# A fused attention and expert kernel: order of ACT's and DVE's work within the attention steps, Newton groups, and the work behind the steps

## The chip, the cores and the metric

The kernel runs on one core of one Trainium2 chip. The metric is the time of the kernel on the device in microseconds (us), taken as the median of several runs. Beside it there is one profiled execution, whose trace gives each instruction's engine, line, start and duration; times in such a trace count from the start of its span. The engines are named as the profile does: PE is TensorE, DVE is VectorE, ACT is ScalarE, POOL is GpSimd, SP issues most of the DMAs.

## What is computed

The input `x` is 16 blocks of 128 tokens with 512 features; `ctx` is 16 blocks of 128 context tokens with 128 features, which serve both as keys and values. There are 32 query heads and 8 key heads of 16 features each, so four query heads share a key head. Then comes a mixture of 32 experts, of which each token takes 8, and a shared expert. Cut to what matters, the reference is:

```python
q = layernorm(x)                                  # no scale, no bias, eps 1e-5
w = softmax(q_heads @ k_heads.T / sqrt(16))       # per block and head
x = x + w @ v_heads                               # keys and values are ctx
h = layernorm(x)
scores = sigmoid(h @ gate_weight.T)               # 32 experts in 8 groups
# the best 4 groups by their two best scores, then the best 8 experts of these,
# weights normalised to sum to 2.5
routed = sum over chosen e: weight_e * (silu(h @ w1_e.T) * (h @ w3_e.T)) @ w2_e.T
x = x + routed + (silu(h @ sw1.T) * (h @ sw3.T)) @ sw2.T
```

All inputs and the output are fp32.

## The kernel before

**Stages.** The attention (`attention_small`) takes the first part of the span; then the routing (`route` and `slot_tokens`) computes weights and token lists while PE does the shared expert; then the experts run one after the other on gathered tokens, and their outputs are added to the output in memory by indirect DMAs. The change touches the attention, the seam between it and the routing, and the two helpers for layer normalisation.

**Order.** The instructions of PE, DVE, ACT and POOL stand in each engine's queue in the order in which the program writes them (`tc.manual_schedule`, around L180). So the place of a call in the Python text is its place in the queue, and an instruction that waits holds up all that stands behind it on its engine. Semaphores between engines are put in by the framework from the tiles that instructions read and write. Two instructions of two engines that touch the same PSUM tile are put in order, also where both only read.

**The steps.** The loop goes over 32 steps n, one for each block b = n // 2 and each half i of its key heads. In step n, in this order:

- what is listed for the head of the step (`head[n]`): among it, at certain steps, the masked copies of keys on ACT (`keys`, L335), the normalised rows of a coming block on DVE (`rows_of`, L118), statistics for the layer norms on DVE (`layernorm_stats`, L91 and L92), Newton iterations for reciprocal square roots (`layernorm_rstd`), the rows for the gate (`gate_rows`, L118, on POOL or DVE, each followed by a DMA of 256 KB on SP's queue to `rows` in memory);
- `scores(n)`: PE multiplies queries and keys into two PSUM tiles `sc` (L442), ACT takes the exponentials to `p` (L452). The pool of `sc` has two buffers, both of which one step fills, so the scores of the next step wait for these exponentials;
- `values(n-1)`: PE multiplies the exponentials and values (L458) into `oT`, of which there is one buffer, and DVE copies it to `oTs` (L467);
- at some steps `gate_parts`: PE (L519) into the single buffer `lg`, ACT copies to `lgTs` (L528);
- `transposes(...)`: PE transposes up to two sets into one PSUM tile `x` of which there is one buffer (L415). The sets are the outputs of step n-2 (`added`), the queries of a coming block (`queries`, at even steps), or gate rows of a finished block (`turn_of`, from step 13 on). Then each set's follow-up is called in the order of the sets. For `added`, which comes first, it is a reciprocal (L476) and a product `at` (L478) on DVE and an addition to the block on POOL (L485); for the other two it is a copy by ACT, to `qT` (L433) or to `xnT` (L496);
- at some steps `gate_sums`: PE (L534) into `lg`, DVE copies to `logits` (L537);
- what is listed for the tail of the step.

At the heads of steps 8, 10, 12 and 14 stand squares of the context on ACT (L355) with a sum over them on DVE (L360); at 21 and 22 the longest key is found and compared with a bound.

**The seam.** After step 31 the last outputs are transposed, divided and added, the last blocks get statistics, Newton iterations, gate rows, transposes, gate parts and sums, in an order written out by hand (L640 to L671). `filler(n)` puts n matmuls of the shared expert (each a 512-column one, two instructions in the profile) between. Then `route` begins with ACT's sigmoid of `logits` (L1088) and 20 more such matmuls on PE, behind which PE counts the selected tokens (L1181).

Of the kernel before, what the change touches and what calls it, by code (L numbers as in the profile page):

```python
# [9 lines left out]
F32 = mybir.dt.float32  # L10
# [36 lines left out]
def tile_xattn_moe(  # L47
# [46 lines left out]
    def layernorm_rstd(first, n, eng=nc.vector):  # L94

        ve = xnp.tile([P, B], F32, tag="ve", name="ve")[:, 0:n]
# [3 lines left out]
            r, ve.bitcast(I32), -0.5, float(0x5F3759DF), ALU.mult, ALU.add  # L100
# [3 lines left out]
        for i in range(3):  # L104
            to = rstd[:, first : first + n] if i == 2 else r
            if eng is nc.vector:
                eng.scalar_tensor_tensor(h, r, -0.5, r, ALU.mult, ALU.mult)
                eng.tensor_tensor(h, h, ve, ALU.mult)
                eng.scalar_tensor_tensor(to, h, 1.5, r, ALU.add, ALU.mult)
            else:  # L110
                eng.tensor_tensor(h, r, r, ALU.mult)
                eng.tensor_tensor(h, h, ve, ALU.mult)
                eng.tensor_scalar(h, h, -0.5, 1.5, ALU.mult, ALU.add)
                eng.tensor_tensor(to, h, r, ALU.mult)
# [22 lines left out]
    FIRST = [*range(12), *range(15, 19)]  # L137
    SECOND = [*range(12, 15), *range(19, 2 * B)]
# [124 lines left out]
    def attention_small():  # L263


        with ExitStack() as ph:
# [86 lines left out]
            def key_lengths(k):  # L353
                sq = kpool.tile([P, 4 * KV, HD], F32, tag="sq", name="sq")
                nc.scalar.activation(  # L355
                    sq.rearrange("p k d -> p (k d)"),
                    cn[:, quarter[k], :].rearrange("p b e -> p (b e)"),
                    AF.Square,
                )
                nc.vector.tensor_reduce(kn[:, k, :], sq, AX.X, ALU.add)  # L360
# [41 lines left out]
            def transposes(*sets):  # L402


                x = ps_x.tile([P, 2, 2, 2, P], F32, tag="x", name="x")
# [18 lines left out]
                for s, (_, _, then) in enumerate(sets):  # L424
                    then(x[:, :, :, s])

            def queries(b):
# [3 lines left out]
                def then(x):  # L431
                    qTs[b] = ap2.tile([P, 2, 2, P], F32, tag="qT", name="qT")
                    nc.scalar.copy(qTs[b], x)  # L433
# [39 lines left out]
            def add(b, i, o):  # L473
# [11 lines left out]
                nc.gpsimd.tensor_tensor(part, part, at, ALU.add)  # L485

            def added(b, i):
# [3 lines left out]
                    lambda x: add(b, i, x.rearrange("p h r (g e) -> p (h r) g e", e=HP)),  # L491
                )

            def turn_of(b):
                def then(x):
                    nc.scalar.copy(  # L496
# [33 lines left out]
            def gate_sums(b):  # L530
                t = parts_of.pop(b)
                lg = ps_lg.tile([P, 2 * P], F32, tag="lg", name="lg2")[:, 0 : 2 * E]
                for i in range(2):
# [3 lines left out]
                nc.vector.tensor_copy(  # L537
                    logits[:, b : b + 2, :], lg.rearrange("p (b e) -> p b e", e=E)
                )
# [5 lines left out]
            head, tail = {}, {}  # L545

            def at_head(n, f, *a):
                head.setdefault(n, []).append((f, a))

            def at_tail(n, f, *a):  # L550
                tail.setdefault(n, []).append((f, a))


            for b in (2, 3):
                at_head(0, layernorm_stats, b, FIRST)
            at_tail(0, layernorm_rstd, 1, 3)
            at_tail(0, rows_of, 1)
            at_tail(1, rows_of, 2)
            for b, n in ((4, 1), (5, 1), (6, 2), (7, 2)):
                at_tail(n, layernorm_stats, b, FIRST)  # L560
            at_head(3, layernorm_rstd, 4, 4, nc.gpsimd)
            for b, n in zip(range(8, B), (5, 7, 8, 9, 11, 13, 14, 15)):
                at_head(n, layernorm_stats, b, FIRST)
            for b in range(3, B):
                at_head(2 * b - 3, rows_of, b)

            at_head(3, fixed_values, 1, nc.gpsimd)
            at_head(4, keys, 1, 0)
            at_head(5, keys, 1, 1)
            at_head(5, values_of, 1)  # L570
# [1091 lines left out]
```

## Time and profile before

| What | Value |
|---|---|
| median of 3 runs | 995.25 us (994.85 to 995.45) |
| the profiled execution's own time | 1000.62 us |
| its span | 998.8 us |
| mean granted PE clock | 0.991 of full speed |
| first scores (step 0) start | 10.49 us |
| scores of step 8, of step 31 start | 34.79 us, 111.21 us |
| sigmoid that begins the routing starts | 136.31 us |
| count of selected tokens starts on PE | 155.77 us |
| first expert's matmuls start | 234.04 us |

To read it: the span is the time between the profile's first and last instruction, and the execution's own time is a little longer. The profile's page first lists how busy each engine was, then the same in 40 slices of the span, here 25 us each, as tenths. Its chain of work follows the last instruction back to what released it, step by step. A line of the timeline is start, length, engine, line of the program, operation, the output and inputs by the program's names, and how many instructions were merged; the idle time ahead of it and what ended it stand in brackets. `PEld` is PE's loading of weights, which overlaps its matmuls. One matmul in fp32 appears as two instructions. A stretch of the windows view lists for each engine the busy time and the number of instructions, then the granted PE clock, the share of the DMA engines and GB/s.

### The profile page before, as it was taken

To read this page: it belongs to the slowest core of one execution; us is meant where nothing else is said; L and a number is where in the kernel's file an instruction comes from. 1 tells how busy PE (TensorE), PEld (TensorE's weight loads), DVE (VectorE), ACT (ScalarE), POOL (GpSimd) and SP (SyncE) were. 2 spreads that over 40 slices of the span, in tenths; PEclk is the share of its full clock that TensorE was granted. 3 is DMA by queue.
4 is the path that set the end of the run, shared out by engine and by line. 5 is a ranking of instruction groups with operands and counts; after the bars stand their busy time and mean duration, and the time that the engine had idled before them with its cause. 6 is when DMAs were issued, how large, how long until landed. Compare 5 with 4: busy or idle time off the path is not lost.

```text
span 998.8 us, 13920 instructions
## 1 busy us (share of the span) xinstructions
PE 972.1 (97%) x4965; PEld 550.6 (55%) x4965; DVE 286.9 (29%) x970; ACT 296.6 (30%) x466; POOL 488.4 (49%) x622
## 2 busy tenths in 40 slices
PE   8999899998999999999999999999999999999996
PEld 5334444545666556676666666667654444444453
DVE  6875668971211112121112111111111111211100
ACT  5777522421222212222222222222222222221221
POOL 3566432753445536444546454545464444455443
PEclk9999999999999999999999999999999999999998
DMA  9010104224767657667767676767675777666533
GB/s 310 19 46 36 61 22 179 65 89 145 171 133 170 139 132 186 144 150 182 160 149 164 152 160 156 163 166 180 133 171 151 154 169 185 144 160 164 120 66 45
DMA packets 59870, 137.16 MB, mean 137 GB/s; under 512 B 12168, under 2 KB 16392, under 8 KB 59792
## 3 DMA queue, kind: packets, MB, share of 16 engines
q0 software_dynamic: 32032, 69.25, 36.3%
q1 hardware_dynamic: 27680, 66.81, 19.7%
q8 instruction: 41, 0.67, 0.3%
q14 instruction: 37, 0.30, 0.1%
q10 hardware_dynamic: 80, 0.13, 0.0%
HBM read 96.71 MB, written 46.73 MB: 144 GB/s over the span
## 4 chain that ended last, share of the span: by engine, by line
PE 88%; issue 3%; POOL 2%; ACT 2%; DMA 1%; DVE 1%; another core or an unknown queue 1%; SPq 0%; POOLq 0%; ACTq 0%; DVEq 0%
PE gu L1474 44%; PE y L1528 22%; PE gu L244 6%; PE sc L442 4%; PE trx L1426 4%; PE oT L458 2%; POOL out_dram L1500 2%; PE y L1321 1%; PE x L415 1%; DMA out_dram<-yw,token 1%; ACT p L452 1%; PE tok L988 1%; DMA cn<-in_c_dram 1%; PE lgT L519 0%
## 5 line engine op out<-in xcount | busy, mean ns | idle before, releaser
L1474 PE MATMUL gu<-xnT,wup 128*128 128x256 f32 (+27 forms) x1664 | 492.1, 446 | 4.0 <-ACT xnT L1442 4.0
L1474 PEld LDWEIGHTS gu<-xnT,wup 128*128 128x128 f32 x1664 | 315.4, 191 | 197.1 <-issue 133.5
L1500 POOL DMA_INDIRECT out_dram<-yw,token x150 | 234.8, 1565 | 352.0 <-ACT yw L1537 245.4
L1528 PE MATMUL y<-wdn,sa 128*128 128x512 f32 (+2 forms) x672 | 263.3, 599 | 0.0
L1485 DVE TENSOR_TENSOR sa<-sl,gu 128x256 f32<-128x256 f32 (+27 forms) x104 | 52.2, 502 | 602.3 <-PE gu L1474 571.4
L1537 ACT ACTIVATE yw<-y,wt 128x512 f32<-128x512 f32 x138 | 94.8, 687 | 250.2 <-PE y L1528 201.5
L1402 POOL DMA_INDIRECT xg<-rows,token x138 | 142.3, 1031 | 47.8 <-issue 28.6
L1528 PEld LDWEIGHTS y<-wdn,sa 128*128 128x128 f32 (+2 forms) x672 | 98.0, 170 | 94.4 <-issue 85.0
L1483 ACT ACTIVATE sl<-gu 128x256 f32<-128x256 f32 (+27 forms) x104 | 46.7, 449 | 240.1 <-PE gu L1474 226.7
L1442 ACT COPY xnT<-trx 128x512 f32<-128x512 f32 x69 | 37.2, 589 | 99.4 <-PE trx L1426 84.8
L452 ACT ACTIVATE p<-sc 128x1024 f32<-128x1024 f32 x64 | 62.2, 1026 | 5.1 <-PE sc L442 4.9
L244 PE MATMUL gu<-xnT,sup 128*128 128x512 f32 x128 | 60.6, 613 | 0.7 <-ACT ssl L252 0.7
L982 POOL TENSOR_SCALAR hq<-slice_q,sq 128x138 f16<-128x138 f16 x32 | 35.2, 1114 | 34.6 <-DVE sq L1287 18.4
L442 PE MATMUL sc<-qT,kz 32*128 32x512 f32 x256 | 47.7, 640 | 4.1 <-ACT p L452 2.5
L1442 DVE COPY xnT<-trx 128x512 f32<-128x512 f32 x57 | 39.3, 689 | 31.7 <-PE y L1528 21.1
L1426 PEld LDWEIGHTS trx<-ident,xg 64*128 64x128 f32 x1104 | 37.2, 139 | 17.8 <-issue 17.5
L485 POOL TENSOR_TENSOR x<-x,at 128x256 f32<-128x256 f32 x32 | 23.3, 730 | 43.8 <-DVE at L478 43.7
L1426 PE MATMUL trx<-ident,xg 64*128 64x64 f32 x1104 | 42.1, 226 | 0.0
L244 PEld LDWEIGHTS gu<-xnT,sup 128*128 128x128 f32 x128 | 23.3, 194 | 24.5 <-issue 21.9
L458 PE MATMUL oT<-p,va 128*32 128x512 f32 x256 | 34.1, 605 | 0.0
L1457 DVE SCALAR_TENSOR_TENSOR own<-expert,owner,xg 128x32 f32<-128x32 f32 x138 | 31.4, 246 | 0.0
L1321 PE MATMUL y<-sdn,sa 128*128 128x512 f32 x64 | 29.3, 595 | 0.0
(186 smaller groups left out, 463.9 us busy)
## 6 DMA issues: line engine op xcount, KB each, us to landing
wup<-in_w_dram SPq DMA_DIRECT2D x64, 512.0 KB
wdn<-in_w_dram SPq DMA_DIRECT2D x32, 512.0 KB
rows<-xn SPq DMA_DIRECT2D x16, 256.0 KB
out_dram<-x SPq DMA_DIRECT2D x16, 256.0 KB
x<-in_x_dram SPq DMA_DIRECT2D x15, 256.0 KB
out_dram<-yw,token POOLq DMA_INDIRECT x150
xg<-rows,token POOLq DMA_INDIRECT x138
cTs<-in_cT_dram SPq DMA_DIRECT2D x4, 256.0 KB
```

The source lines that it names most:

```text
L244: nc.tensor.matmul(acc, lhsT=sup[:, w, d, ts(i, P)], rhs=xnT[k][:, d, :], start=(d == 0), stop=(d == ND - 1),)
L442: nc.tensor.matmul(scs[j // 2][:, j % 2], lhsT=kzs[b // 4 % 2][rows, b % 4, i, :], rhs=qT[rows], start=True, stop=True, tile_position=(j * ...
L452: nc.scalar.activation(p, sc, AF.Exp, scale=1.0 / HD**0.5)
L458: nc.tensor.matmul(oT[j * HP : (j + 1) * HP], lhsT=vas[b // 4 % 2][:, b % 4, 2 * j + i, :], rhs=ps.pop((b, i, j)), start=True, stop=True, ...
L1402: nc.gpsimd.indirect_dma_start(out=t, out_offset=None, in_=rows[:, :], in_offset=bass.IndirectOffsetOnAxis(ap=token[:, j : j + 1], axis=0) ...
L1426: nc.tensor.matmul(trs[s // 2][:, h, s % 2, d, :], lhsT=xg[j][rows_of_half, ts(d, P)], rhs=ident[rows_of_half, rows_of_half], start=True, ...
L1442: copy(xnT[n % NTB][:, :, col : col + P].rearrange("p d (h t) -> p h d t", h=2), tr)
L1474: nc.tensor.matmul(acc[:, 0:m], lhsT=wup[k % NW][:, w, d, ts(i, P)], rhs=xnT[n % NTB][:, d, 0:m], start=(d == 0), stop=(d == ND - 1),)
L1485: nc.vector.tensor_tensor(acts[n % NTB][:, i, 0:m], banks[2][:, 0:m], acc[:, 0:m], ALU.mult)
L1500: ins = nc.gpsimd.indirect_dma_start(out=flat, out_offset=bass.IndirectOffsetOnAxis(ap=token2[:, k - 1 : k] if a else token[0:b, j : j + 1 ...
L1528: nc.tensor.matmul(y[c0:c1, :], lhsT=acts[n % NTB][:, i, col : col + c1 - c0], rhs=wdn[pieces[n][0] % NW][:, i, :], start=(i == 0), stop=( ...
L1537: nc.scalar.activation(yws[j], y, AF.Copy, scale=wt[:, j : j + 1])
```

## The change

It has five parts.

1. In `transposes` the set of `added` comes last, so that ACT's copy of the other set is called first. Ahead of the last set's follow-up a new list, `between`, is run: what the new dictionary `middle` lists for the step. `rows_of` moves there from the heads (block b from the head of step 2b-3 to the middle of step 2b-4), the statistics of blocks 8 to 15 move there (odd steps 3 to 17), and the sums over squares too. In the last step the old order of sets is kept.
2. The copies of the first two blocks' queries go from ACT to DVE.
3. The squares go from steps 8 to 14 to steps 21 to 27; the longest key is found at 30 and compared at 31.
4. `layernorm_rstd` takes two iterations in place of three, with other constants, the second of higher order: on DVE 9 instructions in place of 11, on POOL 12 in place of 14. The groups are dealt out anew: on POOL four at steps 10, 16, 22 and 27 in place of five at 9, 15, 21, 27 and 31; that of step 31 goes to DVE.
5. The seam is written anew. The additions of the last four half blocks go from POOL to DVE, the gate rows of blocks 12 and 13 from DVE to POOL, the copies of the last logits from DVE to ACT, the transposes all go through `transposes` (two sets in a tile, some in a buffer of the `sc` pool), `gate_parts(8)` goes from step 31 behind it, and of the eight fillers two stand ahead of the last sums and six behind, where five and three stood.

```diff
@@ layernorm_rstd
+        c1, c2 = 0.703952253, 0.703952253 * 2.38924456
+        if eng is nc.vector:
+            z = xnp.tile([P, B], F32, tag="z", name="z")[:, 0:n]
+            eng.scalar_tensor_tensor(h, r, -c1, r, ALU.mult, ALU.mult)
+            eng.tensor_tensor(h, h, ve, ALU.mult)
+            eng.scalar_tensor_tensor(r, h, c2, r, ALU.add, ALU.mult)
+
+            eng.scalar_tensor_tensor(h, r, 0.375**0.5, r, ALU.mult, ALU.mult)
+            eng.tensor_tensor(z, h, ve, ALU.mult)
+            eng.scalar_tensor_tensor(h, z, -1.25 / 0.375**0.5, z, ALU.add, ALU.mult)
+            eng.scalar_tensor_tensor(to, h, 1.875, r, ALU.add, ALU.mult)
...
@@ transposes
-            def transposes(*sets):
+            def transposes(*sets, pool=ps_x, between=()):
...
                 for s, (_, _, then) in enumerate(sets):
+                    if s == len(sets) - 1:
+                        for f, a in between:
+                            f(*a)
                     then(x[:, :, :, s])
@@ queries
-                    nc.scalar.copy(qTs[b], x)
+                    (nc.scalar.copy if b > 1 else nc.vector.tensor_copy)(qTs[b], x)
@@ add
-                nc.gpsimd.tensor_tensor(part, part, at, ALU.add)
+                eng.tensor_tensor(part, part, at, ALU.add)
@@ what the steps hold
-            for b, n in zip(range(8, B), (5, 7, 8, 9, 11, 13, 14, 15)):
-                at_head(n, layernorm_stats, b, FIRST)
+            for b, n in zip(range(8, B), range(3, 18, 2)):
+                at(middle, n, layernorm_stats, b, FIRST)
             for b in range(3, B):
-                at_head(2 * b - 3, rows_of, b)
+                at(middle, 2 * b - 4, rows_of, b)
...
             for k in range(NTB):
-                at_head(8 + 2 * k, key_lengths, k)
-            at_head(21, longest)
-            at_tail(21, longest_turned)
-            at_tail(22, compare_lengths)
+                at(head, 21 + 2 * k, squares, k)
+                at(middle, 21 + 2 * k, key_lengths, k)
+            at(head, 30, longest)
+            at(tail, 30, longest_turned)
+            at(head, 31, compare_lengths)
...
-            for n, group in ((9, (8, 7)), (15, (15, 7)), (21, (22, 3)), (27, (25, 3)), (31, (28, 2))):
-                at_head(n, layernorm_rstd, *group, nc.gpsimd)
+            for n, group in ((10, (8, 7)), (16, (15, 6)), (22, (21, 4)), (27, (25, 3))):
+                at(head, n, layernorm_rstd, *group, nc.gpsimd)
+            at(head, 31, layernorm_rstd, 28, 2)
@@ the loop
                 sets = []
-                if n > 1:
-                    sets.append(added(*items[n - 2]))
                 if n % 2 == 0 and 0 < n // 2 < B - 1:
                     sets.append(queries(n // 2 + 1))
                 if n in turned:
                     sets.append(turn_of(turned[n]))
+                if n > 1:
+                    sets.append(added(*items[n - 2], nc.gpsimd if n < N - 1 else nc.vector))
+                if n == N - 1:
+                    sets.reverse()
+                between = middle.get(n, ())
                 if sets:
-                    transposes(*sets)
+                    transposes(*sets, between=between)
@@ the seam
+            for b in (12, 13):
+                gate_rows(b, nc.gpsimd)
+            gate_parts(8)
+            values(*items[N - 1])
+            layernorm_stats(14, SECOND)
+            transposes(added(*items[N - 2], nc.vector), turn_of(11), pool=ps_sc)
...
+            transposes(added(*items[N - 1], nc.vector))
+            layernorm_stats(15, SECOND)
+            layernorm_rstd(SECOND[14], 2)
+            nc.scalar.activation(table, table, AF.Sigmoid)
+            gate_sums(8, nc.scalar.copy)
+            transposes(turn_of(12), turn_of(13))
             gate_parts(10)
             filler(1)
-            gate_sums(10)
+            gate_sums(10, nc.scalar.copy)
...
             filler(1)
             gate_parts(12)
-            filler(2)
             gate_rows(15, nc.vector)
+            transposes(turn_of(15), pool=ps_sc)
             gate_rows(14, nc.vector)
+            transposes(turn_of(14, nc.vector.tensor_copy))
+            gate_sums(12, nc.scalar.copy)
...
             gate_parts(14)
-            gate_sums(14)
-            filler(3)
+            gate_sums(14, nc.scalar.copy)
+            filler(6)
```

## The prediction

> **What bounds the kernel now.** I read the page's engine shares first, then the chain of work that ended last, then the waits of the attention stage and its timeline. The page:
>
> ```profile
> PE 972.1 (97%) x4965; PEld 550.6 (55%) x4965; DVE 286.9 (29%) x970; ACT 296.6 (30%) x466; POOL 488.4 (49%) x622
> ...
> DVE  6875668971211112121112111111111111211100
> ACT  5777522421222212222222222222222222221221
> ```
>
> DVE and ACT are loaded only in the first five slices (125 us), which the change touches; there all engines pass work round within 3 us. TensorE's 97% is no measure of fullness: a matmul that waits in the array counts as busy. The timeline of the end of attention step 4, step 5, and the start of step 6 shows what happens (start, length, engine, line; in brackets idle time and what ended it):
>
> ```profile
> 25.13 0.41 PE L415 MATMUL x<-ident,xq 64*128 64x64 f32 x8
> ...
> 25.58 0.26 DVE L476 RECIPROCAL ri<-x 128x16 f32<-128x16 f32 x1
> ...
> 25.94 0.42 DVE L478 TENSOR_TENSOR at<-x,ri 128x256 f32<-128x256 f32 x1
> 26.46 0.59 ACT L433 COPY qT<-x 128x512 f32<-128x512 f32 x1 [1.28 <-DVE at L478]
> ...
> 26.94 0.72 ACT L335 ACTIVATE kz<-cTs,odd 128x512 f32<-128x512 f32 x1
> ...
> 27.56 1.93 ACT L452 ACTIVATE p<-sc 128x1024 f32<-128x1024 f32 x2
> ...
> 28.63 2.04 PE L442 MATMUL sc<-qT,kz 32*128 32x512 f32 x8 [0.63 <-ACT p L452]
> ```
>
> Step 4's transposes end at 25.54. ACT is free and its copy's data are there, but it waits for DVE's product `at` (end 26.36). The exponentials behind it start late, and the next scores wait for the PSUM that they release and run 2.04 us in place of 1.07. The waits from 8 to 112 us (total, times, longest) say that this is the rule:
>
> ```profile
> DVE oTs L467 <- PE oT L458: 23.2, 16, 3.5
> ACT qT L433 <- DVE at L478: 11.8, 12, 1.4
> ...
> ACT xnT L496 <- DVE at L478: 4.1, 7, 1.0
> ```
>
> Sixteen us of ACT are lost behind `at`; DVE has 23 us of slack in front of `oTs`. In the seam after the steps, the stretches of windows show TensorE's clock halved for 6 us, after TensorE was under half busy from 114.7 to 121:
>
> ```profile
> 114.70:121.00 6.30, 3.00 (x35) 1.73 (x33) 4.18 (x11) 1.36 (x3) 3.18 (x12) 1.00 0.20 73
> ...
> 122.00:125.00 3.00, 2.51 (x13) 1.37 (x14) 0.00 (x0) 1.34 (x3) 0.00 (x0) 0.50 0.02 5
> 125.00:128.00 3.00, 3.00 (x7) 1.58 (x7) 0.64 (x2) 1.55 (x3) 0.00 (x0) 0.50 0.00 0
> ```
>
> From 136.02 (routing) to 212 the chain is TensorE almost without a gap, so there time is TensorE's work.
>
> **What the skill says.** "PSUM — Partial Sum Buffer", Terms: two engines on the same bank and quadrant at once are an error, "reads against reads included". That is why a copy and a product of different halves of one tile are put in order; the trace agrees (copy 0.10 us after `at` ends, each time), so the change can only turn that order round. "TensorE: Matmul & The Clock Gate", HAM oscillation, asks for no idle gaps over about 3.4 us; here the clock fell with gaps of 1.5 us at most, so many short ones do it too. "GPSIMD Engine Reference", Engine selection, calls one-input work on GpSimd roughly line-rate; the trace does not agree: a normalisation is 2085 ns on POOL (x9), 549 to 671 ns on DVE.
>
> **The change, part by part.** *(1) The loop's floor.* From sc(4) at 22.00 to sc(31) at 111.21 are 27 steps in 89.2 us. Their TensorE work at the rate of unstretched rows: scores 1.07 and values 1.00 each (55.9); transposes 0.65 in 23 steps with two sets, 0.40 in 4 with one (16.6); four gate parts of 0.43, four sums of 0.56, one turn of 0.27 (4.2). Together 76.7: 12.5 us are stalls, and more than that cannot come out of these steps.
>
> *(2) Copy first.* It can start 0.07 after the transposes and takes 0.59; the first half of the next scores is ready 0.60 after them, so the exponentials follow at once. In exchange DVE's reciprocal now waits for the copy: `ri` and `at` end at 0.07+0.59+0.09+0.36+0.42 = 1.53 us after the transposes, before 0.82. Behind them on DVE stand the tail's statistics and the next `oTs`; TensorE waits for `at` with the next transposes, which come 2.07 us later. Slack 0.54, if ACT is free when the transposes end. The pieces put between (rows 0.46, statistics 0.82, a key sum 0.68) run in that wait on even steps. On odd steps without a copy they come ahead of `ri`: `at` ends 0.10+0.61 (`oTs`)+0.82+0.36+0.42 = 2.31 us after the transposes began, and the next begin 0.40+2.07 = 2.47 after: no stall, barely. DVE per pair of steps: 2x(0.61+0.36+0.34)+2x0.82+0.46 = 4.7 us; ACT: 4x0.975+0.6 = 4.5, with a second copy 5.1; TensorE 5.19, with two two-set steps 5.44.
>
> Walked pair by pair, with 0.4 for each kz (0.72 us of ACT at heads 4, 5, 9, 11, 17, 19; unchanged) and 5.9 where ACT's sum passes TensorE's (squares, 0.64 each, now at 21 to 27 in place of 8 to 14): steps 8-9 from 6.78 to 5.6, 10-11 from 6.77 to 5.6, 12-13 from 6.31 to 5.4, 14-15 from 7.24 to 5.4 (a square leaves), 16-17 from 6.66 to 6.4, 18-19 from 6.42 to 5.9, 20-21 from 7.99 to 6.4 (`longest`'s stalled turn leaves for 30), 24-25 from 6.79 to 6.4, 28-29 from 6.70 to 6.4, the others nothing. Sum 8.2.
>
> *(3) The start.* qT(0) and qT(1) go to DVE (priced as `oTs`, DVE's copy of 128x512 from PSUM, 0.69). sc(0) could start at 9.1, but the first exponential follows `va`'s copy (its keys' DMA, end 9.96): 1.7 earlier than 11.67. DVE pays 0.69 and saves two Newton operations at a pitch of 0.20; sc(2) comes at about 14.4 (16.39). Then DVE, with eight statistics to do, binds: I walk sc(8) to 32.4 (34.79). Gain 2.4. Bounds: 0 (DVE late) to 2.4. Steps together 10.6; I take 9.3, the rest for handoffs not walked.
>
> *(4) Newton.* POOL 14 to 12 operations at 0.28 (0.56 less, five groups to four, later heads); hidden by POOL's slack of two steps: each `at` waits only for the add two steps back. If that cover goes, 3.3 us of Newton hold up an add, and through it statistics. The group (28,2) leaves POOL (113.01 to 117.09) for DVE: 9x0.20 = 1.8.
>
> *(5) The seam.* From sc(31), t, to the sigmoid at 136.31 were 25.1 us. After: DVE does `at` to t+1.3, statistics of 13 to 2.1, the length check 0.4, Newton 1.8, rows 11 to 4.8, `oTs` to 5.4; values(31) behind that on TensorE to 6.4. The four late adds now run on DVE (0.42 each, `at`'s row of that size; at most the 0.69 of a 128x512 one) in place of POOL 0.73 and its handoff; the last ends at 10.1, statistics 15 at 10.9, Newton at 12.7, rows 15 and 14 at 13.8 (131.6, so t+20.4, before). Rows 12 and 13 go to POOL: 2x2.09, to t+8.5, each with its 256 KB write on SP's queue, order unchanged; behind them on POOL only memsets that wait anyway. ACT, with logits' copies added (0.25 each, between DVE's 0.22 for them and ACT's 0.38 for 256 columns), and the single `lg` buffer give: turn 15 and 14 to 15.9, sums 12 to 15.8, parts 14 to 16.7, sums 14 to 17.8, sigmoid 18.1. A halved clock took 3.3 us from TensorE before (6.6 at half rate, partly beside other waits); I add 1.1, a third, between none and all of it: 19.2, 5.9 us less. But fillers went from five ahead of the sigmoid to two, and six after it in place of three; from there TensorE binds (count started at 155.77, its selection ended at 155.50), so 3x0.87 = 2.6 us come back. Net 3.3; with the clock's bounds 1 to 4.5, and with a us of unwalked waits either way 0 to 5.5.
>
> *(6)* The rest shifts whole: weights, gathers and writes start from routing. Sum 9.3+3.3 = 12.6 us. On the profiled execution's own 1000.62 (span 998.8) that is 988.0; the runs' median is 0.5% less, which changes 12.6 by 0.1. Forecast 995.25-12.6 = 982.7.
>
> **Rivals.** *Half the loop:* the late release of x and DVE's odd steps take TensorE's place as the stall; for it speaks the slack of 0.54 and the near 2.3 against 2.47, against it DVE's 23 us of slack. Loop 4.5 in place of 9.3: 987.5. *Better seam:* TensorE's gaps end sooner, the clock stays up: 1.1 of my allowance, and 2.5 of short waits: 979. *Slower:* ACT runs behind by d when the transposes end, so copy, sums and release of x all slip; TensorE then stalls d-0.54 in each of about 25 two-set steps. It ends slower than before from d = 1.14 us on (0.6x25 = 15, over the 12.6 by 2), a little over one exponential; at d = 1.3 it costs 19: 982.7+19 = 1001.7. ACT's 5.9 against 5.44 in steps 18 to 27 speaks for it, but that backlog is half a us. *No change:* the 13 us gather wait from 219.73 absorbs the gain, if its end is set by DMA and not by the token list: 995. Its transfers start from routing, which speaks against.
>
> **Numbers.** Forecast 0.55, half the loop 0.25, better seam 0.10, slower 0.06, no change 0.04. Faster by over 0.2% (2 us, about what a measurement can tell here) 0.90, same 0.04, slower 0.06. The range reaches from the better seam with the loop's undiscounted 10.6 (977.8, set to 977) to half the loop with the start's 2.4 gone too (989.9): 990.
>
> **What would show it.** The wait of ACT's copies for `at` gone, `ri` waiting for ACT in its place; sc(8) near 32.4, sc(31) near 102, the sigmoid near 121; scores of 1.07 and few of 2.04. Wrong would be: transposes that wait for `at` by over 0.3 us a step, a seam as long as 25 us, or a later gather wait grown by what was won.

## The result and the profile after

The changed kernel takes 985.95 us (median of 4 runs, 985.39 to 987.26), the kernel before on the same chip 995.35 (994.85 to 996.01): a ratio of 0.9907 with a 95% interval of 0.989 to 0.9924, so 9.4 us faster where 12.6 were forecast. The profiled execution took 987.26 us, its span 985.4. The page of the changed kernel, the lines that answer to those of before:

```profile
PE 966.0 (98%) x4985; PEld 548.8 (56%) x4985; DVE 288.7 (29%) x972; ACT 296.7 (30%) x468; POOL 486.6 (49%) x597
...
DVE  7877778961121111111112111111121111111100
ACT  5788513412222222222222222222221222222221
```

Almost nothing was removed: DVE and ACT have as many busy microseconds as before, only closer together in the first five slices. Where the time went is read from landmarks of the traces:

| | before | after | gain | forecast |
|---|---|---|---|---|
| scores of step 8 start | 34.79 | 32.79 | 2.00 | 2.4 |
| from there to the scores of step 31 | 76.42 | 71.17 | 5.25 | 8.2 |
| from there to the sigmoid | 25.10 | 20.86 | 4.24 | 5.9 |
| from there to the count on PE | 19.46 | 22.05 | -2.59 | -2.6 |
| count | 155.77 | 146.87 | 8.90 | |

(The forecast took 9.3 for the first two lines together.) The profiled execution gained another 4.5 us behind the count. That does not belong to the change: from the count to the end of the execution the 14 traces of this study take either 840.3 to 840.5 us or 844.8 to 846.1, and which it is does not go with the edits. In the nine long ones, that of before among them, ACT's first copy for the experts starts 2.9 us after the transposes that it reads instead of at once, TensorE then waits 4.0 to 4.3 us in place of 1.17, and behind this wait its granted clock is at half for 3.4 or 6.8 us. All eight traces taken on two of the chips are long and all four taken on two others short, and the kernel before itself takes 1001.13 and 1000.80 us on the former, 995.68 and 995.79 on the latter; what holds up that copy is open. The medians' 9.4 agree with the 8.9 at the count.

The stretch at steps 4 to 6 that the prediction showed, in the timeline of the changed kernel:

```profile
23.74 0.44 PE L434 MATMUL x<-ident,oTs 64*128 64x64 f32 x8
...
24.22 0.59 ACT L455 COPY qT<-x 128x512 f32<-128x512 f32 x1 [0.26 <-PE x L434]
...
24.70 0.73 ACT L349 ACTIVATE kz<-cTs,odd 128x512 f32<-128x512 f32 x1
...
25.34 1.94 ACT L474 ACTIVATE p<-sc 128x1024 f32<-128x1024 f32 x2
...
25.88 0.24 DVE L498 RECIPROCAL ri<-x 128x16 f32<-128x16 f32 x1
26.15 0.42 DVE L500 TENSOR_TENSOR at<-x,ri 128x256 f32<-128x256 f32 x1
...
26.72 0.46 PE L434 MATMUL x<-ident,oTs 64*128 64x64 f32 x8 [0.48 <-DVE at L500]
...
27.11 1.35 PE L464 MATMUL sc<-qT,kz 32*128 32x512 f32 x8
```

The transposes end at 24.18 and ACT's copy starts 0.04 us later (before: 0.92 after their end, held by `at`). The masked keys and the exponentials follow without a gap, and the scores of the next step come 3.00 us after those of this one, where 3.16 passed before. `at` now ends 2.4 us after the transposes, and the next ones wait 0.48 us for it; in all steps that wait comes twice, 0.7 us together. The waits from 8 to 104 us (total, times, longest) say the same for all steps:

```profile
ACT p L474 <- PE sc L464: 14.7, 22, 1.8
...
PEld sc L464 <- ACT p L474: 4.5, 12, 0.8
...
DVE ri L498 <- ACT qT L455: 3.4, 7, 1.0
...
DVE ri L498 <- ACT xnT L518: 1.0, 3, 0.5
...
PE x L434 <- DVE at L500: 0.7, 2, 0.5
```

ACT's 16 us of waiting for `at` are gone, and DVE waits 4.4 us for ACT in exchange, as forecast. The 16 us did not become 16 us of time: ACT's first line, its wait for scores, grew from 4.9 us to 14.7. What took the place of the old wait is seen in one plain pair of steps:

```profile
88.59 1.14 PE L464 MATMUL sc<-qT,kz 32*128 32x512 f32 x8
...
89.83 1.94 ACT L474 ACTIVATE p<-sc 128x1024 f32<-128x1024 f32 x2 [0.92 <-PE sc L464]
...
91.30 1.65 PE L464 MATMUL sc<-qT,kz 32*128 32x512 f32 x8
...
91.82 0.30 PEld L464 LDWEIGHTS sc<-qT,kz 32*128 32x128 f32 x4 [0.22 <-ACT p L474]
```

The exponentials begin 1.24 us after the scores' start, 0.10 after their end: both halves of the scores come ready together. So the second exponential ends at 91.77, 3.18 after the scores began, and the second half of the next scores, which needs its PSUM, loads at 91.82. TensorE was there at 91.30. The scores last 1.65 in place of 1.07 to 1.14, once in each pair. ACT waits for TensorE, then TensorE for ACT, and neither is full.

In the seam TensorE's clock falls as before, only elsewhere (windows; the column ahead of the last two is the granted clock):

```profile
106.00:109.00 3.00, 1.61 (x28) 0.73 (x24) 2.65 (x15) 1.14 (x2) 0.75 (x2) 1.00 0.00 0
109.00:112.00 3.00, 2.43 (x18) 0.80 (x20) 1.88 (x5) 0.86 (x2) 3.00 (x2) 0.55 0.36 135
...
115.00:118.00 3.00, 2.62 (x26) 1.21 (x27) 2.58 (x13) 2.29 (x6) 0.00 (x0) 0.69 0.02 5
```

The clocks shown are means over the windows. Narrower ones give 0.50 from 109.4 to 112.7 us and again from 116.2 to 119.5, and 1.00 between and beside them; before it is 0.50 from 121.3 to 128.0. So the clock is at half for 6.8 us in both kernels, in two pieces or in one.

### The profile page after: what moved, and what is told of

Same layout as the page of the kernel before. It is cut to its first block, busy times and chain, and to the rows that moved or that the text cites. A ratio compares the mean times of both kernels' runs of the same rounds, so it can differ in the third digit from the quotient of the medians.

```text
span 985.4 us, 13941 instructions
## 1 busy us (share of the span) xinstructions
PE 966.0 (98%) x4985; PEld 548.8 (56%) x4985; DVE 288.7 (29%) x972; ACT 296.7 (30%) x468; POOL 486.6 (49%) x597
## 4 chain that ended last, share of the span: by engine, by line
PE 86%; issue 5%; POOL 3%; DMA 2%; DVE 2%; ACT 1%; POOLq 0%; ACTq 0%; DVEq 0%
PE gu L1492 42%; PE y L1546 21%; PE gu L258 6%; PE trx L1444 4%; PE sc L464 4%; PE oT L480 3%; POOL out_dram L1518 3%; PE y L1339 2%; DMA out_dram<-yw,token 2%; PE x L434 2%; PE warm L329 1%; PE tok L1006 1%; PE lg L556 0%; PE lgT L541 0%; DVE st L91 0%
## 5 line engine op out<-in xcount | busy, mean ns | idle before, releaser
L464 PE MATMUL sc<-qT,kz 32*128 32x512 f32 x256 | 43.9, 640 | 0.2 <-ACT p L474 0.2
L507 POOL TENSOR_TENSOR x<-x,at 128x256 f32<-128x256 f32 x29 | 21.3, 740 | 38.6 <-DVE at L500 36.4
```

The costliest lines, as they stand in the source:

```text
L464: nc.tensor.matmul(scs[j // 2][:, j % 2], lhsT=kzs[b // 4 % 2][rows, b % 4, i, :], rhs=qT[rows], start=True, stop=True, tile_position=(j * ...
```

## The experiments

**First group: which part makes the gain.** The theory was that the order of the sets makes the loop's 5.25 us.

*Order alone.* The kernel before, with:

```diff
                 sets = []
-                if n > 1:
-                    sets.append(added(*items[n - 2]))
...
                     sets.append(turn_of(turned[n]))
+                if n > 1:
+                    sets.append(added(*items[n - 2]))
+                if n == N - 1:
+                    sets.reverse()
```

> The kernel before, with one edit: within a step ACT's copy set is dealt ahead of DVE's sums set (except in the last step). My theory: the order alone gives the loop's gain, steps 8 to 31 get shorter by 5 us (measured 5.25 with the whole change), so the time falls from 995.4 to about 990 (988.5 to 991.5), and ACT's wait for the product at (11.8 and 4.1 us) is gone. Rival: the rows and statistics that the change puts between, and the squares and the length search that it moves to the end, do it; then the order alone gives under 1.5 us (994 to 996), because on DVE the rows and statistics now stand ahead of the late product and hold TensorE's transposes.

*Order undone.* The changed kernel, with:

```diff
-                if n == N - 1:
-                    sets.reverse()
+                if n > 1:
+                    sets = sets[-1:] + sets[:-1]
```

> The changed kernel with DVE's sums set dealt first again in every step, all else as changed. My theory (the order makes the loop's gain): 5 to 7 us come back, 991 to 993, and ACT waits for the product at again by over 8 us between 8 and 104 us. Rival (the moved squares, rows and statistics make it): at most 1.5 us come back, 986 to 987.5.

*First copies alone.* The kernel before, with:

```diff
-                    nc.scalar.copy(qTs[b], x)
+                    (nc.scalar.copy if b > 1 else nc.vector.tensor_copy)(qTs[b], x)
```

> The kernel before with the first two query copies on DVE in place of ACT, nothing else. My theory of the start: the first exponential no longer stands behind two copies of 0.6 us, and sc(8) comes up to 2 us earlier, which stays to the end: about 993.4. Rival: DVE, which has eight statistics to do there, pays 0.69 us for each copy and binds, so that sc(8) comes at the old time or later: 995 to 996; the start's gain in the changed kernel then comes from the other moves (statistics later, shorter Newton groups).

*Seam alone.* The changed kernel with order, first copies and the steps' lists as before:

```diff
-            for b, n in zip(range(8, B), range(3, 18, 2)):
-                at(middle, n, layernorm_stats, b, FIRST)
+            for b, n in zip(range(8, B), (5, 7, 8, 9, 11, 13, 14, 15)):
+                at(head, n, layernorm_stats, b, FIRST)
...
-                at(middle, 2 * b - 4, rows_of, b)
+                at(head, 2 * b - 3, rows_of, b)
...
-                at(head, 21 + 2 * k, squares, k)
-                at(middle, 21 + 2 * k, key_lengths, k)
-            at(head, 30, longest)
-            at(tail, 30, longest_turned)
-            at(head, 31, compare_lengths)
+                at(head, 8 + 2 * k, squares, k)
+                at(head, 8 + 2 * k, key_lengths, k)
+            at(head, 21, longest)
+            at(tail, 21, longest_turned)
+            at(tail, 22, compare_lengths)
```

> The changed kernel with the attention steps as before: sums first, rows, statistics, squares and length search at their old steps, first copies on ACT; what stays of the change is the work behind the last step and the shorter Newton groups. My theory: the seam is worth its 4.2 us less the 2.6 us of fillers behind the sigmoid, so 995.4-1.6 = 993.8 (992.5 to 994.5). Rival: the seam's gain exists only because the steps before it leave DVE less behind; then sc(31) to the sigmoid stays near 25 us and, with 2.6 us of fillers added, the time is 995.4 to 998.

**Second group: what the order needs beside it, and the seam.** *Between undone*: the changed kernel with the first three removed and the first three added lines of the last diff (statistics and rows at their old heads), nothing else.

> The changed kernel with DVE's statistics of the next query blocks and its query rows put back to the heads of their old steps; copies first, squares and length search late, seam as changed. My new theory, after the order alone gained only 0.8 us: the order pays only if these pieces stand behind it; at a step's head they stand ahead of the product that now comes late, and one of them waits for x (at step 7 of the order-alone run the next scores came 2.9 us late). Then the start loses 2 to 3 us again and steps 8 to 31 about 1: 3 to 4 us over the changed kernel, 0.994 of the time before. Rival: the moved squares and length search are the second half of the gain, and the place of rows and statistics costs at most 1 us: 0.991 to 0.992.

*Squares back*: the changed kernel with the rest of that diff, squares and length search at their old steps.

> The changed kernel with the squares, their sums and the length search at their old steps (8 to 14, 21, 22); rows and statistics between, as changed. My theory: in the order-alone run steps 20 to 23 took 15.1 us against 12.6 in the changed kernel, because the search's turn on TensorE waits for DVE behind the late product; so 2 to 2.5 us of the gain come from moving it, less 0.4 that DVE saves behind the last step: 0.9925 of the time before. Rival: with the rows and statistics out of the way the search costs nothing at step 21, and ACT's squares lie as well at 8 to 14: 0.9905, as the changed kernel.

*Fill gaps*: the changed kernel with fillers moved (and the transposes of step 30 given a PSUM buffer ahead of them, so that the order of buffers fits):

```diff
             gate_parts(8)
+            x30 = ps_sc.tile([P, 2, 2, 2, P], F32, tag="sc", name="x")
...
+            filler(2)
             values(*items[N - 1])
             layernorm_stats(14, SECOND)
-            transposes(added(*items[N - 2], nc.vector), turn_of(11), pool=ps_sc)
+            transposes(added(*items[N - 2], nc.vector), turn_of(11), x=x30)
...
             gate_sums(8, nc.scalar.copy)
+            filler(1)
             transposes(turn_of(12), turn_of(13))
...
-            filler(6)
+            filler(3)
```

> The changed kernel with three of the six expert pieces that stand behind the sigmoid put into TensorE's idle stretches of the seam: two ahead of the last values (1.96 us idle there), one ahead of the turns of 12 and 13 (1.35 us idle). My theory: TensorE's work from the sigmoid on sets the end, so 3 x 0.87 = 2.6 us leave it, and the busy array keeps its clock, which gives the last values (1.93 us at the lowered clock, 1.06 in the run with the old steps) and the pieces their full rate: 2.6 to 4 us, 0.9865 to 0.988 of the time before. Rival: the pieces hold up the last values or the turns by their own length on TensorE's queue, and the chain through DVE and ACT to the sigmoid slips by it: 0 to 1 us gain, 0.990 to 0.991.

*Three Newton iterations*: the changed kernel with the old iterations and their constant (`for i in range(3)` with factors -0.5 and 1.5), its groups dealt as changed.

> The changed kernel with the three old Newton iterations in place of the two new ones, so two more small operations per group on DVE and POOL, their dealing as changed. My theory: POOL's are hidden by two steps of slack, and DVE's two groups stand at the start and twice in the seam on the path (0.20 us an operation): 0.4 to 1.2 us over the changed kernel, 0.991 to 0.992 of the time before. Rival: POOL's late rstd holds up the query rows, which now come one step earlier, and the loop loses more than 2 us: above 0.993.

**Third group: what bounds a plain pair.** *A piece ahead* and *a piece between*: in `scores` of the changed kernel, in blocks 4 to 14, with `j == 0` and `j == 1` in turn:

```diff
+                    if 4 <= b < 15 and j == 0:
+                        nc.scalar.copy(table, table)
                     nc.scalar.activation(p, sc, AF.Exp, scale=1.0 / HD**0.5)
```

> The changed kernel with one small ACT copy (0.2 us, a 128x1 table onto itself) ahead of the two exponentials of every step from 8 to 29. My theory of why a plain pair of steps takes 5.92 us and not TensorE's 5.44: the two halves of the scores come ready together, 1.23 us after they start, and the second half of the next scores waits for the second exponential; this is a chain from TensorE to ACT and back, in which ACT waits for the scores (14.7 us in all). A piece ahead of the exponentials falls into that wait: steps 8 to 31 stay within 0.3 us of the changed kernel's 71.2. Rival: ACT's throughput is the bound there, and each of the 22 pieces costs its 0.2 us: 74 to 75.6.

> The same small ACT copy between the two exponentials of every step from 8 to 29. The chain theory: it makes the second exponential 0.2 us later, and with it the second half of the next scores, in each pair that this chain bounds: 0.2 us in each of 6 to 11 pairs, so 72.4 to 73.5 us for steps 8 to 31. Throughput theory: the same as with the piece ahead, 74 to 75.6. If neither, and TensorE alone sets the pace: 71.2 in both.

*Turns between*: the changed kernel, with `scores` calling a function after its second matmul:

```diff
                 for j in range(NJ):
+                    if j == NJ // 2:
+                        between()
...
+            late = range(6, N - 2)
...
+                if n - 1 in late:
+                    scores(*items[n], lambda: turns(n - 1))
+                    rest_of(n - 1)
```

where `turns` holds the sets and the transposes of a step, and `rest_of` what stands behind them.

> The changed kernel with TensorE's transposes of the step before issued between the two halves of the scores of steps 7 to 30, Newton groups and rows on POOL a step later. Chain theory: the transposes fill TensorE's wait for the second exponential, the first exponential finds its half ready sooner, and a plain pair goes from 5.92 toward 5.44: up to 5 us off steps 8 to 31 (66 to 68 us). Rival: the four matmuls of the scores run side by side on four strips of rows; issued as two halves they no longer do, each half takes about the 0.7 us that a half took alone in the order-alone run, and a step gets longer by 0.3 to 1 us: 78 to 95.

**Last: a further version.** *Fill more*: the kernel with the gaps filled, and:

```diff
-                nc.vector.tensor_copy(
+                (nc.scalar.copy if (b, i) in items[-2:] else nc.vector.tensor_copy)(
                     t.rearrange("p g (h s) -> p h g s", h=2),
...
-            filler(1)
+            filler(2)
             transposes(turn_of(12), turn_of(13))
...
             gate_parts(14)
+            filler(1)
             gate_sums(14, nc.scalar.copy)
-            filler(3)
+            filler(1)
```

> The kernel with three pieces in the seam's gaps, and three things more: a second piece ahead of the turns of 12 and 13 (0.53 us idle there), one between the parts and the sums of 14 (0.54 us idle), so that one piece stays behind in place of three, and the copies oTs of the last two steps on ACT, which waits 3.0 us there, in place of DVE, which is busy for 2.5 to 2.8 of every 3 us. My theory: from the last scores to the count TensorE's work is all there is, less its idle time, about 2.0 us of which is left; the two pieces take 1.1 of it and the earlier chain through DVE some of the rest: 1 to 2 us, 0.9842 to 0.9852 of the time before, count at 139.5 to 140.5 us. Rival: each piece delays the chain by what it does not hide and ACT's copies push the copies xnT: 0.986 to 0.988, count at 141.5 or later.

**What they gave.** Times are ratios to the kernel before on the same chip, with their 95% intervals (0.001 is 1 us); the other columns are landmarks of the traces in us.

| run | ratio | sc(8) | sc(8) to sc(31) | to sigmoid | to count |
|---|---|---|---|---|---|
| before | 1 | 34.79 | 76.42 | 25.10 | 19.46 |
| after | 0.9907 (0.989, 0.9924) | 32.79 | 71.17 | 20.86 | 22.05 |
| order alone | 0.9992 (0.9983, 1.0001) | 36.26 | 74.62 | 25.71 | 19.46 |
| order undone | 0.998 (0.9969, 0.9991) | 33.59 | 77.86 | 19.17 | 22.05 |
| first copies alone | 0.9986 (0.9976, 0.9995) | 33.63 | 76.71 | 25.50 | 19.45 |
| seam alone | 0.995 (0.9934, 0.9966) | 34.31 | 76.39 | 19.16 | 22.05 |
| between undone | 0.9909 (0.9894, 0.9925) | 33.40 | 71.54 | 19.94 | 22.05 |
| squares back | 0.9915 (0.9899, 0.9931) | 32.72 | 74.18 | 22.27 | 22.04 |
| fill gaps | 0.9862 (0.9841, 0.9883) | 32.54 | 71.18 | 18.27 | 19.48 |
| three Newton | 0.9913 (0.9897, 0.9929) | 32.93 | 71.18 | 20.08 | 22.04 |
| a piece ahead | 0.9911 (0.9891, 0.9932) | 32.02 | 71.28 | 19.49 | 22.05 |
| a piece between | 0.991 (0.9893, 0.9926) | 32.06 | 71.75 | 20.99 | 22.05 |
| turns between | 1.0113 (1.0096, 1.013) | 32.65 | 90.40 | 20.36 | 22.05 |
| fill more | 0.9859 (0.984, 0.9878) | 32.13 | 71.18 | 18.18 | 19.56 |

The first column of landmarks moves with the start of the first step (8.80 to 9.56 us in the runs with the first copies on DVE). The second repeats to 0.03 us where nothing in these steps differs, but for the first copies alone, where it is 0.3 longer than before.

**The order needs company.** The expectation for the order alone fell: 0.8 us and not 5, as the rival beside it had it. Undone in the changed kernel it costs 7.3 us by the ratios (0.998 less 0.9907, some 2 either way) and 5.8 at the count, where 5 to 7 were expected, and ACT's copies `qT` wait 16.0 us for `at` again. Both are true, since the order alone opens two stalls that the rest of the change removes. The first is at step 7 of the order-alone run (timeline):

```profile
27.24 1.74 PE L442 MATMUL sc<-qT,kz 32*128 32x512 f32 x8
...
27.84 0.69 DVE L91 BATCH_NORM_STATS2 st<-x 128x6 f32<-128x512 f32 x1 [1.70 <-POOL x L485]
...
28.67 0.66 DVE L91 BATCH_NORM_STATS2 st<-x 128x6 f32<-128x512 f32 x1
...
29.46 0.51 DVE L118 TENSOR_SCALAR xq<-x,mv,rstd 128x512 f32<-128x512 f32 x1
29.89 0.68 DVE L467 COPY oTs<-oT 128x512 f32<-128x512 f32 x1
...
30.63 0.16 PEld L458 LDWEIGHTS oT<-p,va 128*32 128x32 f32 x8 [2.48 <-DVE oTs L467]
30.63 1.28 PE L458 MATMUL oT<-p,va 128*32 128x512 f32 x8 [1.65 <-DVE oTs L467]
...
32.89 2.04 PE L442 MATMUL sc<-qT,kz 32*128 32x512 f32 x8
```

Two statistics and a row stand ahead of `oTs` on DVE, and the first of them waits 1.70 us for POOL's addition. So the copy comes no sooner than before (29.89 against 29.83), though the scores come 1.39 us sooner; the values of the step wait for that copy, TensorE idles 1.65 us, and then its clock is at half (0.50 in a window from 31.4 to 34.7). 5.65 us pass from one step's scores to the next. With between undone the same pieces stand there, TensorE idles 1.14 us, the clock stays at 1.00, and it is 4.53. The other is at step 21, in the run with the squares and the search put back (timeline):

```profile
77.69 0.27 PE L387 MATMUL kT<-ident,km 128*1 128x128 f32 x1 [1.24 <-DVE logits L559]
...
79.40 1.94 PE L480 MATMUL oT<-p,va 128*32 128x512 f32 x8
```

The search's turn shares the single `lg` buffer with the sums, whose copy stands on DVE behind the product `at`, now late. TensorE idles 1.24 us there (0.41 in the kernel before, where `at` came early), and then its clock is lowered: the granted clock is 1.00 until 78.4 us, 0.50 from 78.6 to 81.8 and 1.00 again from 82.0, and values that take 1.06 us take 1.94. Steps 8 to 31 lose 3.0 us by it, 2.55 of them in steps 20 to 23. In the traces the moved squares and search are thus the second half of the loop's gain, as the rival in the second group had it; the place of statistics and rows is worth 0.4 us in steps 8 to 31 and 0.7 at the start (sc(8) less sc(0) 23.89 in place of 23.23). I had expected 3 to 4 from that, which the measured 0.9909 excludes. And the moves need the order: with the sums first they make steps 8 to 31 slower than before (77.86 against 76.42). By the traces, then, in steps 8 to 31 the order is worth 1.8 us in the kernel before and 6.7 in the changed one; all that the change moves beside it costs 1.4 under the old order and brings 3.5 under the new (74.62 less 71.17). But the trace with the squares back is of the slowest of its eight runs: 997.33 us at a mean clock of 0.987, where the median is 992.6 and five of the others had 0.992 or 0.993. By the ratios the search's place is 0.8 us with an interval of some 2 either way, so how much of the 3.0 us the other runs lost is open.

**The start.** The first copies alone give 1.4 us (0.5 to 2.4), of which the traces show 0.7 to 1.2 at sc(8), by which run of the old start it is set against (34.31 or 34.79). The steps 0 to 8 themselves stay as long (24.31 against 24.30): what the edit brings is an earlier first step (sc(0) at 9.32; 10.01 to 10.49 in the three runs with ACT's copies). The other us comes with the order: 24.29 from sc(0) to sc(8) without it, 23.23 with it. It needs the shorter Newton iterations too: with three it is 23.76, since DVE's row at step 5 then waits 1.16 us for POOL's group in place of 0.63, and the step takes 3.53 us in place of 3.00.

**The seam.** Alone it is worth 3.35 us at the count (5.94 less 2.59) and 5.0 by the ratio (3.4 to 6.6), against 1.6 expected. It takes 19.16 us to the sigmoid. In the changed kernel it takes longer, with the same instructions behind the last step. The values of the last step, first in the changed kernel, then with the seam alone:

```profile
109.57 1.93 PE L480 MATMUL oT<-p,va 128*32 128x512 f32 x8 [1.96 <-DVE oTs L489]
```

```profile
115.44 1.06 PE L480 MATMUL oT<-p,va 128*32 128x512 f32 x8 [1.07 <-DVE oTs L489]
```

They start 5.61 us after the last scores in the one and 4.74 in the other, since ACT's copy first puts step 30's `at` later on DVE, and the last length check comes there too; and they run at half the clock or not. How the clock falls differs among executions: with the same idle 1.96 us ahead, they took 1.93, 1.06, 1.07 and 1.49 us in four traces (after, between undone, a piece ahead, a piece between), and the way to the sigmoid 20.86, 19.94, 19.49 and 20.99. In all 14 traces the clock is full or half, and up to the count a half stretch lasts 3.4, 6.8 or 10.2 us. Each of the 18 falls there follows 3.4 us in which TensorE was busy for 0.41 to 0.64 of the time; no stretch with a greater share was followed by one, but six with a share up to 0.64 were not either. The half stretches of a trace begin on one grid of 3.4 us; where it lies against a gap differs among the traces, which may be why the same gap lowers the clock now and not then. No run tests that.

Filling the gaps does what it was meant to. Its timeline and a window:

```profile
107.31 1.98 PE L258 MATMUL gu<-xnT,sup 128*128 128x512 f32 x4
...
109.24 1.07 PE L481 MATMUL oT<-p,va 128*32 128x512 f32 x8
```

```profile
109.00:112.00 3.00, 2.74 (x37) 1.48 (x36) 2.79 (x8) 0.86 (x2) 3.00 (x2) 1.00 0.44 165
```

The two pieces end where the values could begin, the clock stays at 1.00 from 100 to 127 us, the sigmoid comes 2.59 us sooner after the last scores and the count 2.57 sooner after the sigmoid, which is the three pieces. That is 4.5 us better than the changed kernel by the ratios and 5.4 at the count, about twice the 2.6 of the pieces themselves: the other half is the shorter way to the sigmoid, with the clock kept up.

Filling more gave nothing that can be measured, 0.3 us. The count after it:

```profile
141.05 0.55 PE L1204 MATMUL count<-ones,sel 128*32 128x1 f16 x16 [1.27 <-DVE sel L1196]
```

TensorE now waits 1.27 us for DVE's selection. From the sigmoid to the count are 19.5 us in each kernel with three pieces or one behind the sigmoid, and 22.05 in each with six. The two pieces that left are idle time now, and the sigmoid itself came only 0.1 us sooner after the last scores.

**The plain pair.** Throughput of ACT is not the bound: 22 added pieces cost 0.1 us in all ahead of the exponentials and 0.6 between, where it would have been 2.8 or more by the expectation, and 1.8 if each took the 0.08 us that is read below. But the piece was a poor probe, as the timeline of the run with the piece between shows:

```profile
89.50 1.02 ACT L476 ACTIVATE p<-sc 128x1024 f32<-128x1024 f32 x1 [0.77 <-PE sc L464]
...
90.42 0.18 ACT L475 COPY table<-table 128x1 f32<-128x1 f32 x1
90.50 1.03 ACT L476 ACTIVATE p<-sc 128x1024 f32<-128x1024 f32 x1
```

The second exponential starts 1.00 us after the first, with the piece of 0.18 us overlapped; without it the two start 0.92 apart and take 1.94. So against the first the second exponential moved by 0.08 and not by 0.2. The first begins 1.17 us after the scores in place of 1.24, so that against the scores the second's end moved by 0.03, and a pair by 0.03 too (5.95 against 5.92), less than the 0.2 expected. With the piece ahead the exponentials begin 1.18 us after the scores (why sooner in both is open), and a pair takes 5.86. In all three runs the pair follows the end of the second exponential, 3.18, 3.20 and 3.12 us after the scores, to within 0.01. That fits the chain from TensorE to ACT and back; three points of so small a spread are a weak test of it.

The stronger one is against my remedy. In the run with turns between (TensorE's timeline):

```profile
56.12 1.13 PE L466 MATMUL sc<-qT,kz 32*128 32x512 f32 x4
57.18 1.06 PE L482 MATMUL oT<-p,va 128*32 128x512 f32 x8
58.17 1.13 PE L466 MATMUL sc<-qT,kz 32*128 32x512 f32 x4
```

Half the scores (x4) take 1.13 us and the whole (x8) 1.14. The four matmuls, each on its own 32 rows of the array, run side by side; issued in halves they take that time twice, and the 23 steps get 0.84 us longer on average (19.2 in 23). The chain can't be shortened by cutting the scores, and the halves can't come ready one after the other while they run side by side.

## Why the prediction was right, and where it was off

*Sign and order of size were right*, and 985.95 lies within 977 to 990. The parts were further off than the sum: 3.0 us too much in the loop, 0.4 at the start and 1.7 in the seam, of which the 1.3 taken off for handoffs not walked covered a part by luck, since it names no place. The mechanism in (2) is seen in the waits: `at` no longer holds ACT, `ri` waits for ACT. The floor (1) held: 71.2 us for steps 8 to 31 is still above it. (6) held: the first transposes of the experts come 73.5 us after the count in all 14 traces, so the gather wait absorbed nothing. (What the chain of before shows there as a wait is ACT's; TensorE works until 229.99.)

*(2) The failed step is "the first half of the next scores is ready 0.60 after them, so the exponentials follow at once".* They follow 1.23 to 1.24 us after the scores' start, in the trace of before too, where I had not looked for it:

```profile
82.96 1.14 PE L442 MATMUL sc<-qT,kz 32*128 32x512 f32 x8
...
84.19 1.94 ACT L452 ACTIVATE p<-sc 128x1024 f32<-128x1024 f32 x2 [0.94 <-PE sc L442]
```

By that chain a plain pair takes 5.92 and not 5.4. The pairs from 8 to 15, walked at 5.6, 5.6, 5.4 and 5.4, took 5.87, 5.92, 6.17 and 5.92: 1.9 of the missing 3.0 us. Pair 16-17, with masked keys and a gate part, took 6.92 in place of 6.4 (6.66 before), as additions come on top of 5.92 and don't hide in it. That pairs 22-23 and 26-27 already took 5.92 before, and stood in my walk as pairs with nothing to gain, was the sign that another bound lies there.

*What I had right without its weight:* the length search leaving step 21. I took it at 1.6 us in pair 20-21 (measured 1.36), but under the new order it is 3.0 in the trace with the squares back, because its stall grows there and the clock falls. Order alone shows the same fall (0.51 in a window from 84 to 86 us); by the ratios the 3.0 are not settled.

*(3) Start:* 2.0 of 2.4; the first copies themselves gave about half of it. *(4) Newton:* hidden from step 8 on, as said: three iterations leave 71.18 us where two leave 71.17. At the start the cover fails: there the two operations that POOL saves are worth 0.5 us in step 5. In the seam its two more operations lengthen the wait of the last values from 1.96 to 2.35, twice 0.20; by the ratio 0.6 us, which the interval doesn't tell from nothing.

*(5) Seam:* here the term that was mis-sized is the clock. Without it the walk came to 18.1, and with the gaps filled, where the clock stays full, the way takes 18.27. I allowed 1.1 us for the clock, and in the changed kernel it costs some 2.6 (20.86 less 18.27), 0.87 of them in the last values alone. That the seam alone takes 19.16, next to the forecast's 19.2, is luck: its values start 4.74 us after the last scores, while the walk, with `oTs` done at 5.4, is that of the new order (5.61). The six fillers behind the sigmoid cost 2.59 against 2.6. *Rivals:* "half the loop" came closest, 7.25 for loop and start together lying between its 4.5 and the 9.3, but not for its reason: DVE's odd steps held. The slower case did not show; the clock, which I had only in the seam, did in runs where one part of the change is missing.

## What to carry to other kernels

An order in a queue and the places of the pieces around it are one decision: here the order alone brought 0.8 us, the moved pieces under the old order cost steps 8 to 31 1.4 us, and both together took 5.25 off them, so look for what stands behind the instruction that is made late. Before walking steps to a new bound, look for steps that have no stall of the old kind, and ask why they take longer than the sum of the busiest engine's work. Independent matmuls put into gaps that a dependent chain leaves are worth more than their own length where they keep the clock up, until another engine's chain sets the end.

## What the runs showed of the hardware

- Four fp32 matmuls of 512 columns on four strips of 32 rows take 1.14 us together, and two of them 1.13: they end together, and a reader of the first gains nothing from being first.
- Short stalls lower TensorE's clock: after 1.24 us of idle time it was at half for 3.4 us, after 1.96 us it fell in some executions at once and in others later. In the 14 traces it was full or half, and up to the count half for 3.4, 6.8 or 10.2 us at a time, each time after 3.4 us in which TensorE was busy for 0.41 to 0.64. The seam's way to the sigmoid took 19.5 to 21.0 us in executions with the same instructions in it.
- A small ACT copy of 0.18 to 0.2 us between two long ones takes about 0.08 us of the queue (their starts are 1.00 us apart in place of 0.92).
